# Token lists kept in DRAM instead of one-hot matmuls, in a kernel of linear attention and a mixture of experts on Trainium2

## The chip, the cores and the metric

The kernel runs on one core of one Trainium2 chip. A core has engines that run side by side, each working through its own instructions in order: TensorE (PE, with its weight load PEld) for matmuls, VectorE (DVE), ScalarE (ACT) and GpSimd (POOL) for elementwise work, and SyncE (SP), which here only issues DMAs. POOL issues the indirect DMAs, those whose row addresses come from a list. The metric is device microseconds (us) for one launch. Three runs of the kernel before have a median of 1033.31 us (1033.22 to 1034.61).

## What is computed

The input is 16 sequences of 512 tokens, each of D = 256 numbers. Every token is normalised (`xn`) and goes through two blocks, whose outputs are added to the input:

```
q, k = elu(xn @ Wq + bq) + 1, elu(xn @ Wk + bk) + 1      # 16 heads of 16
v = xn @ Wv + bv
attn = (q @ (k^T v) / max(q . sum(k), eps)) @ Wo + bo     # no softmax: linear
shared = swiglu(xn @ w_in.T) @ w_out.T                    # HIDDEN = 512
g_idx = argmax(softmax(xn @ wg.T + gb))                   # one of 2 groups
w_se = top 2 of the 4 experts of that group, by softmax, times the group's probability
h = swiglu(xn @ w1.T)
routed = sum over experts e of  h * w_se[:, e] @ w2[e].T  # two terms are not zero
out = x + attn + shared + routed
```

Each token thus needs one pair of experts out of 12 (six pairs in each of two groups), and two weights.

## The kernel before

**Two phases.** A loop over the 16 sequences computes all but the routed sum. For each token it leaves one row in `h_d` in DRAM: first the 512 numbers of h, then `BASE` = 258 more (input, attention and shared part added up, then the token's two weights); 770 words in all (`ROW`). Then the tiles phase (class `Tiles`, from L931) takes tokens that share a pair of experts, 128 at a time. `rows()` gathers their rows from `h_d` by an indirect DMA (L943), `turn()` transposes the h part (`hb` on ACT, L964; `hT` on DVE, L970 and L976), `sums()` multiplies by both experts' `w2` at once (`py`, L993), adds with the weights (`y`, L1000 and L1003) and scatters the rows to the output (L1006). Up to 75 tiles (`TILES`) may be needed for 8192 tokens in 12 pairs; 67 (`SURE`) are always run, the others only where a pair's count asks for it, which these inputs do not. Tiles go in twos.

**The homes of gathered rows.** The big buffers of the first phase, `qq_all`, `x_all`, `kk_all` and `xn_all`, are used in turn for the rows of two tiles. The first three of them are free before the last sequence ends. So the rows of the first `AHEAD` = 3 twos are gathered early (from 768.48 us), when h is there but the other part of the last sequence's rows is not. When the last store of `gather_last` has landed (795.13 us), all these rows are gathered once more, whole: two twos ahead of the loop over tiles, the third at its first step, behind the rows for `xn_all`.

**One sequence.** In the order of the code for sequence b: `front(b+1)` makes the residual (`res`, POOL, L390), projects keys, queries and router logits (`pk` L412, `pq` L423) and routes (L433 to L515; DVE, with small pieces on POOL). Routing leaves in `hot` a mark for the token's pair, and in `ahead_of` (POOL) a running count for each partition and pair. Then come `summarize` (`pxk` L689), `normalize` of sequence b+2 (its transposed form goes through DRAM: SP stores `xn_d`, loads four blocks `xb`, L258), `hidden_rows` (`phr`, L595: 14 products, by a scheme of seven per half), `key_sum` (`k` and `k2` on POOL, L676 and L677; `pks` on PE, L679), `attend` (`rz`, L748, and `qb`), `hidden` (`phs`, which ends in `hs_all`), `values` and `mix` (`pvk` L708, `pm` L731, `kvo`), and `gather`: four `po` (L768) of twelve matmuls each, added into `res` by DVE (L777) and stored by SP into the rows of `h_d`.

**What sets the order.** A scheduler places instructions on each engine by their dependencies and priorities; some steps are pinned (`keep_in_program_order`, `issue_after`, `high_priority`). The last sequence pins its `pvk` and `pm` between the products of `hidden` (`small_sums`, L697, with a bank of the pool `ps_y`).

**The order of the tokens** is made by the generator `order()` (L806 to L924), which `between()` (L517) steps forward inside sequences 14 and 15. From the counts it works out where each pair's run of tiles starts, then for every token its slot: tile and row in it. To turn slots into lists it makes one-hot marks on DVE, eight token tiles at a time, and multiplies them on PE, adding up in one bank `pi`:

```python
nc.vector.tensor_tensor(lo, count..., row_of..., ALU.is_equal)       # 128 rows
nc.vector.tensor_tensor(at_tile, count..., tile_of..., ALU.is_equal) # 75 tiles
...
tc.keep_in_program_order(nc.tensor.matmul(
    pi, lhsT=los[:, g % 4, t, :], rhs=his[g % 3][:, t].rearrange("p i n -> p (i n)"),
    start=(g + t == 0), stop=(g * TG + t == TT - 1),
))
```

These are 64 matmuls in bf16 (L894) in eight groups. From `pi` come `source` and `goal`, the row to read and to write for each slot, `where` (which experts each tile takes) and `filled`.

Of the kernel before, what the change touches and what calls it, by code (L numbers as in the profile page):

```python
# [10 lines left out]
FP = mybir.dt.float32  # L11
# [10 lines left out]
def block_kernel(  # L22
# [50 lines left out]
    BASE = D + 2  # L73
    ROW = HID + BASE

    SURE, STEP = 67, 4
    AHEAD = 3
    TG = 8
    TR = 5
    assert TT % TG == 0  # L80
# [10 lines left out]

    h_d = dram.tile([TT * P, ROW], FP, name="h_d")

# [101 lines left out]
    def load_expert(i):  # L195
# [21 lines left out]
    before = const.tile([P, P], FP)  # L217
    nc.gpsimd.affine_select(
        out=before, in_=ones, pattern=[[1, P]],
# [4 lines left out]
    for j in range(EG):  # L224
        nc.gpsimd.memset(place[:, :, j : j + 1], float(j))
    BF = mybir.dt.bfloat16
    count = const.tile([P, P], BF)
    nc.gpsimd.iota(count, pattern=[[1, P]], base=0, channel_multiplier=0,
                   allow_small_or_imprecise_dtypes=True)
    number = const.tile([P, TT], BF)  # L230
    nc.gpsimd.iota(number, pattern=[[1, TT]], base=1, channel_multiplier=0,
                   allow_small_or_imprecise_dtypes=True)
    row = const.tile([P, 1], FP)
    nc.gpsimd.iota(row, pattern=[[0, 1]], base=0, channel_multiplier=1,
# [150 lines left out]
    def residual(b):  # L385

        res = work.tile([P, NT, BASE], FP, tag="res", name=f"res_{b}")
        xt = xs.pop(b)
        for t in range(NT):
            nc.gpsimd.tensor_tensor(res[:, t, 0:D], xt[:, t, :], bo_sb, ALU.add)  # L390
        return res
# [41 lines left out]
    def route(b, lg, res):  # L433
# [75 lines left out]
        for i in range(2):  # L509
            nc.vector.tensor_reduce(  # L510
                res[:, :, D + i : D + i + 1],
                parts[:, i].rearrange("p (t g) c -> p t (g c)", g=G), AX.X, ALU.add,
            )
# [3 lines left out]
    def between(b, n):  # L517

        if b + 2 >= B:
            for _ in range(n or 0):  # L520
                next(steps_of_order)
# [68 lines left out]
    def hidden_rows(b, xs7, then):  # L590
# [16 lines left out]
        seven(f"phr_{b}", product, lambda a: a, room, done, lambda n: between(b, then(n)))  # L607
# [89 lines left out]
    def small_sums(b, shape, name):  # L697

        if b + 1 == B:
            return ps_y.tile(shape, FP, tag="py", name=f"{name}_{b}"), tc.keep_in_program_order  # L700
        return ps_mm.tile(shape, FP, tag="mm", name=f"{name}_{b}"), lambda step: step
# [25 lines left out]
    def mix(b, vk):  # L727
# [7 lines left out]
        with tc.high_priority() if b + 1 == B else nullcontext():  # L735
            nc.scalar.copy(kvo, pm)
# [22 lines left out]
    def outputs(b, t, qT, kvo, hs):  # L759
# [6 lines left out]
        parts += [(qT[:, c, ts(t, P)], kvo[:, c, :]) for c in range(KD)]  # L766
        for i, (a, w) in enumerate(parts):
            nc.tensor.matmul(po, lhsT=a, rhs=w, start=(i == 0), stop=(i == len(parts) - 1))  # L768
        return po

    def gather(b, res, qT, kvo, hs, placed, then):

        for t in range(NT):
            po = outputs(b, t, qT, kvo, hs)

            with tc.issue_after(placed.ins) if placed and t > 1 else nullcontext():
                nc.vector.tensor_tensor(res[:, t, 0:D], po, res[:, t, 0:D], ALU.add)  # L777
            nc.sync.dma_start(out=h_d[ts(b * NT + t, P), HID:ROW], in_=res[:, t, :])
            between(b, then(t))

    def gather_last(b, res, qT, kvo, hs):
# [15 lines left out]
        for i, po in enumerate(pos):  # L797
            to = res[:, 2 * i : 2 * i + 2, 0:D]
# [7 lines left out]
    def order():  # L806

        I32, U32 = mybir.dt.int32, mybir.dt.uint32
        total = keep.tile([P, NP], FP)
        nc.vector.tensor_copy(total, ahead_of[:, TT, :])  # L810
        pc = ps_mm.tile([P, 2 * NP], FP, tag="mm", name="pc")
        tc.keep_in_program_order(
            nc.tensor.matmul(pc[:, 0:NP], lhsT=before, rhs=total, start=True, stop=True)
        )
        nc.tensor.matmul(pc[:, NP:], lhsT=ones, rhs=total, start=True, stop=True)
        pcs = keep.tile([P, 2 * NP], FP)
# [3 lines left out]
        nc.vector.tensor_scalar(ci, pcs[:, NP:], float(P - 1), None, ALU.add)  # L820
# [5 lines left out]
        nc.vector.tensor_copy(runs[0][:, PAD:], ci)  # L826
        for i, d in enumerate((1, 2, 4, 8)):
# [3 lines left out]

        off = keep.tile([P, NP], FP)
        nc.vector.tensor_tensor(off, pcs[:, 0:NP], starts, ALU.add)
        sl = one.tile([P, TT, NP], FP, tag="low", name="sl")
        nc.vector.tensor_tensor(
            sl, ahead_of[:, 0:TT, :], off.unsqueeze(1).to_broadcast([P, TT, NP]), ALU.add
        )
        nc.vector.tensor_tensor(sl, sl, hot, ALU.mult)
        slot = keep.tile([P, TT], I32)
        slf = keep.tile([P, TT], FP)  # L840
        nc.vector.tensor_reduce(slf, sl, AX.X, ALU.add)
        nc.vector.tensor_copy(slot, slf)
        part = keep.tile([P, 2, TT], I32)
        nc.vector.tensor_scalar(part[:, 0, :], slot, P - 1, None, ALU.bitwise_and)
        nc.vector.tensor_scalar(part[:, 1, :], slot, 7, None, ALU.arith_shift_right)
        place_of = keep.tile([P, 2, TT], BF)
        nc.vector.tensor_copy(place_of, part)
# [12 lines left out]
        nc.vector.tensor_copy(where, of)  # L860
        yield


        pi = ps_y.tile([P, 2 * TILES], FP, tag="py", name="pi")

        los = x_all.rearrange("p b t d -> p (b t d)").bitcast(BF).rearrange("p (n t j) -> p n t j", t=TG, j=P)
        his = [
            a[:, B % 2].rearrange("p t d -> p (t d)").bitcast(BF)[:, 0 : TG * 2 * TILES].rearrange(
                "p (t i n) -> p t i n", t=TG, i=2
            )  # L870
            for a in (qq_all, kk_all, xn_all)
        ]

        def marks(g):
            row_of, tile_of = (place_of[:, i, ts(g, TG)].unsqueeze(2) for i in range(2))
            lo, hi = los[:, g % 4], his[g % 3]
            nc.vector.tensor_tensor(
                lo, count.unsqueeze(1).to_broadcast([P, TG, P]), row_of.to_broadcast([P, TG, P]),
                ALU.is_equal,
            )  # L880
            at_tile = one.tile([P, TG, TILES], BF, tag="at_tile", name=f"at_tile_{g}")
            nc.vector.tensor_tensor(
                at_tile, count[:, 0:TILES].unsqueeze(1).to_broadcast([P, TG, TILES]),
                tile_of.to_broadcast([P, TG, TILES]), ALU.is_equal,
            )
            nc.vector.tensor_tensor(
                hi[:, :, 0, :], at_tile,
                number[:, ts(g, TG)].unsqueeze(2).to_broadcast([P, TG, TILES]), ALU.mult,
            )
            nc.vector.tensor_scalar(hi[:, :, 1, :], at_tile, row, None, ALU.mult)  # L890

        def add(g):
            for t in range(TG):
                tc.keep_in_program_order(nc.tensor.matmul(  # L894
                    pi, lhsT=los[:, g % 4, t, :], rhs=his[g % 3][:, t].rearrange("p i n -> p (i n)"),
                    start=(g + t == 0), stop=(g * TG + t == TT - 1),
                ))


        for g in range(TT // TG + 2):  # L900
            if g > 1:
                add(g - 2)
                yield
            if g < TT // TG:
                marks(g)
                yield
        pis = keep.tile([P, 2, TILES], FP)
        nc.vector.tensor_copy(pis.rearrange("p i n -> p (i n)"), pi)
        free = keep.tile([P, TILES], FP)
        nc.vector.tensor_scalar(free, pis[:, 0, :], 0.0, float(2 * TT * P), ALU.is_equal, ALU.mult)  # L910
        tok = keep.tile([P, TILES], FP)
        nc.vector.scalar_tensor_tensor(
            tok, pis[:, 0, :], float(P), pis[:, 1, :], ALU.mult, ALU.add
        )
# [6 lines left out]
        nc.vector.tensor_scalar(source, tok, float(-P), 0.0, ALU.add, ALU.max)  # L921
        goal = keep.tile([P, TILES], U32)
        nc.vector.scalar_tensor_tensor(goal, tok, float(-P), free, ALU.add, ALU.add)
# [5 lines left out]
    rows_of = [a.rearrange("p a b c -> p (a b c)") for a in (qq_all, x_all, kk_all, xn_all)]  # L929

    class Tiles:  # L931
# [6 lines left out]
        def rows(self):  # L938
# [8 lines left out]
            return self  # L947

# [33 lines left out]
        def sums(self):  # L982

            for j, i in enumerate(self.tiles):
# [7 lines left out]
                for f in range(KH):  # L992
# [5 lines left out]
                base = self.hg[:, j, HID:ROW]  # L998
                y = work.tile([P, D], FP, tag="y", name=f"y_{i}", bufs=4)
                nc.vector.scalar_tensor_tensor(  # L1000
                    y, py[:, 0, :], base[:, D : D + 1], base[:, 0:D], ALU.mult, ALU.add
                )
                nc.vector.scalar_tensor_tensor(  # L1003
                    y, py[:, 1, :], base[:, D + 1 : D + 2], y, ALU.mult, ALU.add
# [29 lines left out]
    for b in range(B):  # L1034
# [4 lines left out]
        if b + 2 == B:  # L1039
# [4 lines left out]
            steps_of_order = order()  # L1044
        if b + 1 == B:
            sums7 = token_sums(b, xnT)
            hidden_rows(b, sums7, {2: 2, 6: 2, 9: 2, 13: 2}.get)
# [3 lines left out]
            *lists, filled = next(steps_of_order)  # L1051
            tiles = [Tiles(list(range(i, min(i + 2, SURE))), *lists) for i in range(0, SURE, 2)]
        xk = summarize(b, xn, kk)
# [9 lines left out]
        elif b + 1 < B:  # L1063
            sums7 = token_sums(b, xnT)
            hidden_rows(b, sums7, {9: 1}.get)
# [5 lines left out]
        if b + 2 == B:  # L1071
            next(steps_of_order)
# [3 lines left out]
        if b + 1 < B:  # L1076
            hs, made = hidden(b, sums7) if b else first_hidden(xnT)
            kvo = mix(b, values(b, xk, ksb))
# [11 lines left out]
        if b + 2 == B:  # L1090
            next(steps_of_order)
# [5 lines left out]
        else:  # L1097
            gather(b, res, qT, kvo, hs, normed[b + 2][2]() if b + 2 < B else None, {0: 2, 1: 2, 3: 2}.get)
# [8 lines left out]

# [57 lines left out]
```

## Time and profile before

| | us |
|---|---|
| median of three runs | 1033.31 |
| profiled execution | 1033.23 |
| its span, first to last instruction | 1031.5 |
| granted TensorE clock in it, mean | 0.998 |
| first stage, 0 to 31.5: PE busy | 23.9 |
| sequences 2 to 13, 121.3 to 692.07: PE busy | 569.4 of 570.8 |
| after the last matmul, 1023 to 1031.5: PE busy | 0 |

The span and the profiled execution differ by 1.73 us, which lie around the instructions. The profile gives for each engine its busy time, and for each idle stretch what ended it. A line names the source line, the output, the inputs, their tile and how often. Busy times of matmuls are pipelined: one instruction's duration (mean 592 ns for `py`) is longer than the distance to the next, so what a matmul costs its engine is read from the starts of its neighbours. The clock of TensorE is full in every stage until the tail, so differences of time are not differences of clock.

DMAs move 116.08 MB. The store of `res` (60 of 129 KB) lands 1.9 us after its issue, the four `xb` loads of a sequence 2.8 us after theirs, and the scatter of `y` by POOL 3.0 us after.

### The profile page before, as it was taken

To read this page: it belongs to the slowest core of one execution; us is meant where nothing else is said; L and a number is where in the kernel's file an instruction comes from. 1 tells how busy PE (TensorE), PEld (TensorE's weight loads), DVE (VectorE), ACT (ScalarE), POOL (GpSimd) and SP (SyncE) were. 2 spreads that over 40 slices of the span, in tenths; PEclk is the share of its full clock that TensorE was granted. 3 is DMA by queue.
4 is the path that set the end of the run, shared out by engine and by line. 5 is a ranking of instruction groups with operands and counts; after the bars stand their busy time and mean duration, and the time that the engine had idled before them with its cause. 6 is when DMAs were issued, how large, how long until landed. Compare 5 with 4: busy or idle time off the path is not lost. (4 is left out here: it accounts for less than half of the span.)

```text
span 1031.5 us, 12407 instructions
## 1 busy us (share of the span) xinstructions
PE 1004.9 (97%) x3704; PEld 681.7 (66%) x3704; DVE 779.4 (76%) x1974; ACT 488.1 (47%) x893; POOL 254.8 (25%) x359
## 2 busy tenths in 40 slices
PE   7999999999999999999999999999899999999996
PEld 5466868677786868686777768686667344444442
DVE  5978687878778787878787877868975776666663
ACT  3525353535445253535343534425136576766671
POOL 5302020111202021110202020201012766555652
PEclk9999999999999999999999999999999999999999
DMA  7063534525152522314141313221235755555440
GB/s 220 16 177 107 141 104 101 147 59 154 51 163 54 161 84 81 122 42 143 37 128 56 110 55 123 72 77 61 62 110 146 225 172 153 147 156 157 150 147 30
DMA packets 130339, 116.08 MB, mean 113 GB/s; under 512 B 72637, under 2 KB 114109, under 8 KB 130272
## 3 DMA queue, kind: packets, MB, share of 16 engines
q1 hardware_dynamic: 120064, 77.43, 25.7%
q0 software_dynamic: 9392, 37.58, 12.2%
q8 instruction: 31, 0.51, 0.2%
q10 hardware_dynamic: 816, 0.27, 0.2%
q14 instruction: 36, 0.29, 0.1%
HBM read 65.36 MB, written 50.27 MB: 112 GB/s over the span
## 5 line engine op out<-in xcount | busy, mean ns | idle before, releaser
L993 PE MATMUL py<-w_sb,hT 128*128 x536 | 230.7, 592 | 1.7 <-DVE hT L976 1.6
L993 PEld LDWEIGHTS py<-w_sb,hT 128*128 128x128 f32 x536 | 101.7, 190 | 130.1 <-issue 129.1
L768 PE MATMUL po<-wout_sb,hs_all 128*128 128x256 f32 x480 | 116.6, 380 | 1.4 <-DVE hs_all L580 1.4
L390 POOL TENSOR_TENSOR res<-x_all,bo_sb 128x256 f32<-128x256 f32 x64 | 48.5, 792 | 274.4 <-DMA h_d<-res 203.4
L768 PEld LDWEIGHTS po<-wout_sb,hs_all 128*128 128x128 f32 x480 | 89.2, 190 | 15.1 <-DVE hs_all L580 3.4
L1006 POOL DMA_INDIRECT out<-y,goal x67 | 67.8, 1012 | 76.3 <-DVE y L1003 65.3
L676 POOL TENSOR_TENSOR k<-kk_all 128x512 f32<-128x512 f32 x16 | 20.9, 1307 | 258.3 <-DVE sm L458 247.7
L777 DVE TENSOR_TENSOR res<-po,res 128x256 f32<-128x256 f32 x60 | 25.4, 424 | 76.6 <-PE po L768 76.5
L398 ACT ACTIVATE km<-km 128x1024 f32<-128x1024 f32 x16 | 16.9, 1057 | 138.7 <-DVE km L397 134.4
L595 PE MATMUL phr_w<-w_sb,ss 128*128 128x512 f32 x120 | 61.5, 594 | 2.2 <-DVE ss L538 1.9
L768 PE MATMUL po<-kvo,qT 128*128 128x256 f32 x240 | 61.7, 383 | 0.0
L621 PE MATMUL phs_w<-ss,win_sb 128*128 128x256 f32 x240 | 61.6, 379 | 0.0
L621 PE MATMUL phs_t<-xnT,win_sb 128*128 128x256 f32 x240 | 61.6, 379 | 0.0
L595 PE MATMUL phr_t<-w_sb,xnT 128*128 128x512 f32 x120 | 61.3, 593 | 0.0
L595 PE MATMUL phr_t<-w_sb,ss 128*128 128x512 f32 x120 | 59.4, 597 | 0.0
L621 PE MATMUL phs_t<-ss,win_sb 128*128 128x256 f32 x240 | 59.1, 379 | 0.0
L689 PE MATMUL pxk<-kk_all,xn_all 128*128 128x256 f32 x256 | 58.0, 379 | 0.0
L412 PE MATMUL pk<-wkr_sb,xnT 128*128 128x266 f32 x240 | 57.2, 387 | 0.0
L423 PE MATMUL pq<-w_sb,xnT 128*128 128x256 f32 x240 | 54.2, 379 | 0.0
L689 PEld LDWEIGHTS pxk<-kk_all,xn_all 128*128 128x128 f32 x256 | 48.5, 190 | 6.7 <-issue 0.2
L964 ACT COPY hb<-qq_all 32x256 f32<-32x256 f32 x108 | 43.4, 402 | 17.1 <-DMA qq_all<-h_d,source 9.7
L412 PEld LDWEIGHTS pk<-wkr_sb,xnT 128*128 128x128 f32 x240 | 45.4, 190 | 8.0
(216 smaller groups left out, 1966.0 us busy)
## 6 DMA issues: line engine op xcount, KB each, us to landing
h_d<-hr SPq DMA_DIRECT2D x64, 256.0 KB, 2.5
q_d<-qq_all SPq DMA_DIRECT2D x16, 512.0 KB, 2.8
qb<-q_d SPq DMA_DIRECT2D x64, 128.0 KB, 3.1
w_sb<-in_w SPq DMA_DIRECT2D x64, 128.0 KB, 3.5
h_d<-res SPq DMA_DIRECT2D x60, 129.0 KB, 1.9
x_all<-in_x SPq DMA_DIRECT2D x15, 512.0 KB, 4.8
xn_d<-xn_all SPq DMA_DIRECT2D x14, 512.0 KB, 3.9
xb<-xn_d SPq DMA_DIRECT2D x56, 128.0 KB, 2.8
```

What stands on the lines that cost most here:

```text
L390: nc.gpsimd.tensor_tensor(res[:, t, 0:D], xt[:, t, :], bo_sb, ALU.add)
L412: nc.tensor.matmul(pk, lhsT=xnT[:, k, ts(t, P)], rhs=wkr_sb[:, k, :], start=(k == 0), stop=(k == KD - 1),)
L423: nc.tensor.matmul(pq[:, t, :], lhsT=xnT[:, k, ts(t2 + t, P)], rhs=wq_sb[:, k, :], start=(k == 0), stop=(k == KD - 1),)
L595: tc.keep_in_program_order(nc.tensor.matmul(to, lhsT=xs7[i][:, ts(u, P)], rhs=w1_in[W7[i]], start=start, stop=stop, skip_group_check=True,))
L621: tc.keep_in_program_order(nc.tensor.matmul(split(to)[:, f, :], lhsT=win_in[W7[i]][:, ts(2 * u + f, P)], rhs=xs7[i], start=start and f == ...
L676: nc.gpsimd.tensor_tensor(k2, kk[:, 0:2, :], kk[:, 2:4, :], ALU.add)
L689: nc.tensor.matmul(pxk[:, c, :], lhsT=xn[:, t, ts(c, P)], rhs=kk[:, t, :], start=(t == 0), stop=(t == NT - 1),)
L768: nc.tensor.matmul(po, lhsT=a, rhs=w, start=(i == 0), stop=(i == len(parts) - 1))
L777: nc.vector.tensor_tensor(res[:, t, 0:D], po, res[:, t, 0:D], ALU.add)
L964: nc.scalar.copy(there[ts(q, Q), a - near, 0:n, :], self.hg[ts(a, Q), 0:n, ts(q, W)])
L993: nc.tensor.matmul(py.rearrange("p j d -> p (j d)"), lhsT=self.hT[:, f, ts(j, P)], rhs=w2_sb[:, f, bass.ds(regs[i % TR], 2 * D)], start=(f ...
L1006: stored = nc.gpsimd.indirect_dma_start(out=out_rows, out_offset=bass.IndirectOffsetOnAxis(ap=self.goal[:, i : i + 1], axis=0), in_=y, in_ ...
```

## The change

**Lists by pair, kept in DRAM while the loop runs.** `lists_d` holds, for each of the 12 pairs, 64 rows of 128 entries, and some rows beyond; an entry is one 4-byte word with the token's number, with seven unused words after it. `clear_lists()` fills them once, after sequence 0's `hidden`, with a number beyond all tokens: one memset on POOL and seven DMAs on SP. `enlist(b)` gives every token of a sequence its rank among the tokens of its pair, by two small bf16 matmuls (`pr`), turns it into an address on DVE, and POOL puts each token's number there, 128 at a time. It is called for the next sequence after `attend`, in sequences 1 to 14; the lists of sequences 0 and 1 are made in 1 and 2. The arrays `before` and `ones_bf`, its left operands, are bf16.

**The order.** `order()` is now called at the end of sequence 14. From the counts (`pc`, one bf16 matmul) it works out for each tile which row of `lists_d` it is, gathers these 75 rows (4 KB each) with one indirect DMA, takes every eighth word and transposes the result on PE. Marks, slots, the 64 matmuls and `between()` are gone.

**Sequence 14** places `pvk` and `pm` as sequence 15 does, and its `po` begin with the attention's part.

**Rows** hold the weights first, then the other 256 numbers, then one word of padding (`ROW` = 771 = 3 × 257), so that their last third can be gathered alone. POOL clears the padding in each sequence.

**A fifth home,** `hs_all`, takes rows in turn. The second gathers of the first three twos take only the last 257 words of each row (`bases()`), and stand behind the rows for `xn_all` and `hs_all`.

The core of the diff:

```diff
+    def enlist(b):
+        pr = ps_y.tile([P, NT, NP], FP, tag="py", name=f"pr_{b}")
+        flat = pr.rearrange("p t c -> p (t c)")
+        mine = hot[:, ts(b, NT), :]
+        nc.tensor.matmul(flat, lhsT=before, rhs=mine.rearrange("p t c -> p (t c)"), start=True, stop=False)
+        nc.tensor.matmul(
+            flat, lhsT=ones_bf, rhs=ahead_of[:, ts(b, NT), :].rearrange("p t c -> p (t c)"),
+            start=False, stop=True,
+        )
+        rk = small.tile([P, NT, NP], FP, tag="rk", name=f"rk_{b}")
+        nc.vector.tensor_tensor(rk, pr, lists_at.unsqueeze(1).to_broadcast([P, NT, NP]), ALU.add)
+        nc.vector.tensor_tensor(rk, rk, mine, ALU.mult)
+        rf = small.tile([P, NT], FP, tag="rf", name=f"rf_{b}")
+        nc.vector.tensor_reduce(rf, rk, AX.X, ALU.add)
+        spot = small.tile([P, NT], U32, tag="spot", name=f"spot_{b}")
+        nc.vector.tensor_scalar(spot, rf, float(WORDS), None, ALU.mult)
+        for t in range(NT):
+            put = nc.gpsimd.indirect_dma_start(
+                out=entries,
+                out_offset=bass.IndirectOffsetOnAxis(ap=spot[:, t : t + 1], axis=0),
+                in_=ids[:, b * NT + t : b * NT + t + 1], in_offset=None,
+            )
...
     def small_sums(b, shape, name):
-        if b + 1 == B:
+        if b + 2 >= B:
             return ps_y.tile(shape, FP, tag="py", name=f"{name}_{b}"), tc.keep_in_program_order
...
     def outputs(b, t, qT, kvo, hs):
...
+        if b + 2 == B:
+            parts = parts[KH:] + parts[:KH]
...
     def order():
+        pc = ps_y.tile([P, NP], FP, tag="py", name="pc")
+        nc.tensor.matmul(pc, lhsT=ones_bf, rhs=ahead_of[:, TT, :], start=True, stop=True)
...
+        got = work.tile([P, P * WORDS], U32, tag="blocks", name="got")
+        nc.gpsimd.indirect_dma_start(
+            out=got[0:TILES, :], out_offset=None, in_=lists_d,
+            in_offset=bass.IndirectOffsetOnAxis(ap=part[0:TILES, :], axis=0),
+        )
+        tokens = keep.tile([P, P], FP)
+        nc.vector.tensor_copy(
+            tokens[0:TILES, :], got[0:TILES, :].rearrange("p (n w) -> p n w", w=WORDS)[:, :, 0]
+        )
         yield
-        def marks(g):
...
-        def add(g):
...
+        pi = ps_y.tile([P, TILES], FP, tag="py", name="pi")
+        nc.tensor.transpose(pi, tokens[0:TILES, :], ident[0:TILES, 0:TILES])
...
+    rows_of.append(hs_all.rearrange("p a b -> p (a b)"))
...
+        def bases(self):
+            for j, i in enumerate(self.tiles):
+                nc.gpsimd.indirect_dma_start(
+                    out=self.hg[:, j, HID + 2 :], out_offset=None,
+                    in_=h_d.rearrange("r (a w) -> (r a) w", w=LAST),
+                    in_offset=bass.IndirectOffsetOnAxis(ap=lasts[:, i : i + 1], axis=0),
+                )
...
+        if 0 < b < B - 1:
+            enlist(b + 1)
...
+            if b == 0:
+                clear_lists()
+            elif b < 3:
+                enlist(b - 1)
...
+    EARLY = len(rows_of) - 1
+    for w in tiles[AHEAD:EARLY]:
         w.rows()
     for g, w in enumerate(tiles):
-        if g + AHEAD < len(tiles):
-            tiles[g + AHEAD].rows()
+        if g + EARLY < len(tiles):
+            tiles[g + EARLY].rows()
...
         if g == 0:
-            tiles[AHEAD - 1].rows()
+            for v in tiles[:AHEAD]:
+                v.bases()
```

## The prediction

> **What bounds the kernel now.** I read the busy times first, then TensorE's waits, then busy time by stage, then the timelines of single stages.
>
> The page opens with the span and each engine's busy time, share and count:
>
> ```profile
> span 1031.5 us, 12407 instructions
> ...
> PE 1004.9 (97%) x3704; PEld 681.7 (66%) x3704; DVE 779.4 (76%) x1974; ACT 488.1 (47%) x893; POOL 254.8 (25%) x359
> ```
>
> TensorE is idle for 26.6 us only. 7.6 us are the loading at the start (31.5 − 23.9 busy in the first 31.5 us), 8.5 us the tail after its last matmul. What is left sits mostly in three places. The view of TensorE's waits names them (total, times, longest, in us):
>
> ```profile
> PE pm L731 <- DVE rz L748: 2.5, 1, 2.5
> PE phr_w L595 <- DVE ss L538: 1.9, 1, 1.9
> PE py L993 <- DVE hT L976: 1.6, 1, 1.6
> PE po L768 <- DVE hs_all L580: 1.4, 5, 0.3
> ```
>
> The first two are in sequences 14 and 15, where the order is made; the third is in the tiles phase. Busy time by stage (stage, length, then PE, PEld, DVE, ACT, POOL busy) for sequence 14, for 15, for the tiles:
>
> ```profile
> 692.07:744.50 52.43, 49.73 (x223) 38.06 (x222) 47.67 (x117) 17.33 (x27) 6.23 (x10) 1.00 0.18 58
> 744.50:789.80 45.30, 43.06 (x203) 32.22 (x201) 34.74 (x66) 21.67 (x45) 5.80 (x6) 1.00 0.45 128
> 789.80:1023.00 233.20, 230.71 (x537) 101.50 (x536) 149.90 (x361) 153.78 (x386) 132.00 (x133) 1.00 0.50 152
> ```
>
> An undisturbed sequence is 47.35 us: from pks at 667.24 to the next at 715.03 are 47.79, of which 0.45 are pc. Stage 14 takes 5 us more, with DVE at 47.67 of 52.43 us: it makes the one-hot marks there. So time is won where TensorE executes less, or where DVE stops being late for it.
>
> **What goes.** TensorE's timeline (start, duration, line, operands, count) around pc and the first group of pi:
>
> ```profile
> 711.15 0.29 PE L813 MATMUL pc<-total,before 128*128 128x12 f32 x2
> 711.29 0.37 PE L815 MATMUL pc<-total,ones 128*128 128x12 f32 x2
> 711.51 1.10 PE L595 MATMUL phr_w<-w_sb,ss 128*128 128x512 f32 x2
> ...
> 735.49 0.69 PE L894 MATMUL pi<-qq_all,x_all 128*128 128x150 bf16 x8 [0.23 <-DVE qq_all L890]
> 736.02 1.50 PE L768 MATMUL po<-wout_sb,hs_all 128*128 128x256 f32 x6
> ```
>
> 1. The 64 matmuls of pi: a group of 8 occupies 736.02 − 735.49 = 0.53 us, not 8 times its pipelined duration. Eight groups are 4.3 us, plus about 0.05 each on the instruction behind, 0.4: **−4.7**.
> 2. pc in fp32: 711.51 − 711.15 = 0.36, and 0.09 on the phr pair behind (0.95 against 0.86): 0.45. The single bf16 matmul that replaces it lies between one pi spacing, 0.07, and half of this row, 0.22; I take 0.13, near pi for its type: **−0.3**.
> 3. Waits that the marks and route cause in sequences 14 and 15: pm 2.47 (goes twice over: DVE is freed, and pvk and pm of sequence 14 move later, as 15 has them), phr_w 1.91, one more of phr 0.33, pi 0.23: **−4.9**. What is late next there is hs_all, which holds five po's for 1.4 us in all; it stays.
> 4. The 1.59 us before py of the fourth tile pair. Now its rows come after four whole second gathers; then they are issued first (795.13, in place of 800.15), and second gathers of 257 words stand behind. DVE's order has three y's in front of those transposes, and they wait for these second gathers: by the spacing of 1.25 us the x ones are issued at about 802.7, land 4.3 us later (795.13 to 799.43 below), so y is through at 807.9, the transposes (1.78 + 1.1) at 810.8; TensorE asks at 810.5. About 0.4 is left: **−1.2**.
>
> Sum **−11.1**.
>
> **What comes.**
>
> 5. 16 times pr, two bf16 matmuls of 48 columns with their weight loads. Below, two spacings of the pi row, 2 × 0.067 = 0.13; above, the fp32 pc row, 0.45. I take 0.22, near pi since the type is that: **+3.5** (2.1 to 7.2). Here a rule is weighed: the Trainium skill's "TensorE: Matmul & The Clock Gate", section "Back-to-back issue gap", gives about 81 ns for each load and matmul of 128 columns in a sustained stream, so 32 would be 2.6. A pair alone between fp32 work doesn't overlap like a stream, so I stay above it; a run of the changed kernel will tell.
> 6. The order's new chain. pc now comes after the last phs of sequence 14; some twenty DVE operations of 12 to 60 columns follow, a gather of 75 rows of 4 KB, a copy, and a transpose on TensorE that stands between po_3 of sequence 14 and the first phr of 15. Put on sequence 13's times (last phs at 679.75): offsets done at 686–687, gather 4.3, copy 0.25, so ready at 690.4–691.4. TensorE has four po's of 2.59 and pc: free at 690.2. Wait **+0.8** (0; or 6.6, if the landing takes the 9.9 us that is the longest of such a gather in the trace). The transpose itself: **+0.35** (as pt).
> 7. Sequence 1: the queue of SP now has the store of res_1, which waits for po, before the transfers of xb for sequence 3. Its xnT is then ready about 122.5 by my count of the queue, pk wants it at 121.75: **+0.8** (0 to 2, most of the 2.45 us that one such transfer takes). Queued behind on SP are also the eight w2 loads, wanted much later.
> 8. pm of sequences 1 and 2 stands two matmuls earlier: 0.15 each, **+0.3**.
>
> Sum **+5.75**.
>
> **Costed at nothing.** Four DVE operations of 0.19 us per sequence for rank and address, 0.75 us: DVE has 0.33 + 0.44 + 0.42 = 1.19 us idle at 674–677; behind, from 677.4 to 684.9, it has none, and po waits for it. Without that cover, 14 × 0.75 = 10.5. The 64 puts of 128 entries: POOL issues a gather every 1.25 us, so 5 us per sequence, with POOL idle 75%; behind them stands only k of the next sequence, which pks needs at 667.24 and which is ready at 656.08: 11 us of slack. A put waits for its address on POOL; behind it the same k. Clearing 3.2 MB by seven DMAs: SP is idle from 79.6 to 95.7 us. The word of padding per row and its memset: POOL, idle. Some normalising operations of later sequences move ahead on DVE and one table load on ACT; both engines do the same work in all.
> Against the puts speaks a rule of the skill, "DMA: Bandwidth & Descriptors", section "Anatomy of one DMA — SWDGE (gpsimd) path": a fixed 2.0 us for each DMA, 128 us for 64 if serial. The trace's nearest row, the scatter of y, occupies POOL for 1.01 us each and lands after 3.0; nobody waits for a put until the list is read 30 us after the last. By either price nothing is on the path.
>
> **The sum.** −11.1 + 5.75 = −5.35. The profiled execution took 1033.23 (span 1031.5 and 1.73 around it); the median of the three runs, 1033.31, is the same within 0.1. Forecast **1027.9 us**. Less: pr at 2.1, no wait for the list, none for xb: −8.4, 1024.8. More: the three high ends of 5, 6 and 7 add 3.7 + 5.8 + 1.2 and give 1038.6; together they are unlikely.
>
> **Rivals.**
>
> A, **slower**: a put disturbs DVE. In sequence 14 a POOL operation and a small DVE one ran together:
>
> ```profile
> 701.28 1.31 POOL L676 TENSOR_TENSOR k<-kk_all 128x512 f32<-128x512 f32 x1 [3.17 <-DVE sm L458]
> ...
> 701.62 1.02 DVE L467 TENSOR_TENSOR pe<-ex,sm 128x32 f32<-128x32 f32 x1
> ```
>
> That pe takes 0.18 elsewhere: 0.84 lost. If each of four puts costs DVE 0.8, and its slack is 1.19, then 3.2 − 1.19 = 2.0 us in each of 14 sequences: +28, about 1055. It decides from 1.6 us of delay per sequence, two such hits (14 × 0.4 eats the gain). The skill's "SBUF — State Buffer" says that DVE and GpSimd share a port pair under an exclusive lock and the loser blocks; by this, puts could hurt. Against it, an indirect DMA beside a DVE operation with two SBUF inputs:
>
> ```profile
> 769.82 0.97 POOL L943 DMA_INDIRECT qq_all<-h_d,source  x1 [0.30 <-issue]
> ...
> 769.96 0.42 DVE L722 TENSOR_TENSOR vk<-vk,headmask 128x256 f32<-128x256 f32 x1
> ```
>
> It took 0.42, as at 682.28 with POOL idle. The put is of this kind, so I cost it at zero. A part of A is that the 0.75 us doesn't fit in DVE's gaps.
>
> B, **no change**: the list lands late, +5.8, or pr costs 0.55 each, +5.3: about 1033. For: the longest landing is 9.9. Against: the queue of POOL is nearly empty then, and the gather that these lines show took 4.3 from its issue to the y that waited for it:
>
> ```profile
> 795.13 0.95 POOL L943 DMA_INDIRECT qq_all<-h_d,source  x1 [19.32 <-DMA h_d<-res]
> ...
> 799.43 0.48 DVE L1000 SCALAR_TENSOR_TENSOR y<-py,qq_all 128x256 f32<-128x256 f32 x1 [7.80 <-DMA qq_all<-h_d,source]
> ```
>
> C, **larger gain**: pr at two spacings, no wait for the list: 1024.5. For: both are lower bounds that rows show. Against: the DVE chain has to be done within 7 us with no slip.
>
> That the change doesn't do what it says is excluded: in the instruction order of the changed kernel the 64 matmuls of pi and their marks are gone.
>
> **How the numbers follow.** Forecast 0.60, C 0.10, B 0.11, A 0.19. A measurement of this kernel tells changes over about 0.2%, 2.1 us. Faster: forecast and C, 0.70. Same: B, 0.11. Slower: A, 0.19. The range leaves out the far part of A (above 1036, about 0.14) and a little below: 1024.0 to 1036.0, which takes in C, B and the mild part of A.
>
> **What would show it.** Step 1: no pi group, and stage 14 near 47 us. Step 3: pm and phr_w gone from the waits. Step 4: hT's wait under 0.6. Step 5: the spacing from pr's start to the matmul behind it, 0.22. Step 6: a wait of pi for tokens under 2 us. Step 7: a wait of pk near 122 us. A: waits of po for hs_all, or of pks for k2, that repeat in every sequence, and DVE rows whose means grow. The forecast is wrong if such repeated waits exceed 0.4 us per sequence, or the list lands over 6 us late.

## The result and the profile after

The changed kernel takes 1035.95 us (median of twelve runs, 1034.69 to 1037.52), the kernel before, beside it on the same chip, 1033.99: a ratio of 1.0018, with a 95% interval of 1.0009 to 1.0026. A second comparison gave 1.0017 (1.0010 to 1.0023). So the change costs about 1.9 us, where 5.4 us of gain were forecast.

The page of the changed kernel opens with the span and the busy times:

```profile
span 1033.4 us, 12508 instructions
...
PE 1002.8 (97%) x3670; PEld 680.0 (66%) x3670; DVE 768.4 (74%) x2001; ACT 480.9 (47%) x887; POOL 323.8 (31%) x442
```

TensorE executes 2.1 us less than before and DVE 11 us less; POOL is busy 69 us more (the puts take 72). The span is 1.9 us longer all the same. Where that lies shows when both executions are cut at the same work. The rows give the stage, its length, then PE, PEld, DVE, ACT and POOL busy, clock, DMA share and GB/s. The cuts are the key sum of sequence 2, that of sequence 14, the first `py`, the first `y` of the last tile, and the end. Before:

```profile
0.00:96.47 96.47, 87.18 (x300) 56.70 (x301) 76.78 (x239) 37.37 (x57) 29.83 (x78) 1.00 0.42 120
96.47:667.24 570.77, 569.36 (x2330) 431.58 (x2329) 452.24 (x1165) 249.23 (x367) 79.93 (x131) 1.00 0.35 101
667.24:789.84 122.60, 117.66 (x541) 91.91 (x540) 100.31 (x212) 47.72 (x86) 12.03 (x16) 1.00 0.31 94
789.84:1022.24 232.40, 230.67 (x537) 101.48 (x535) 149.13 (x360) 153.74 (x386) 132.00 (x133) 1.00 0.50 152
1022.24:1031.50 9.26, 0.00 (x0) 0.00 (x0) 0.96 (x2) 0.00 (x0) 0.98 (x1) 0.74 0.03 11
```

After:

```profile
0.00:96.95 96.95, 87.50 (x301) 57.08 (x302) 77.01 (x239) 37.28 (x57) 30.71 (x83) 1.00 0.51 140
96.95:674.65 577.70, 572.88 (x2358) 433.08 (x2357) 466.08 (x1221) 242.37 (x361) 139.09 (x199) 1.00 0.38 102
674.65:786.89 112.24, 112.24 (x479) 87.92 (x478) 76.02 (x183) 47.49 (x86) 21.76 (x26) 1.00 0.38 105
786.89:1017.13 230.24, 230.20 (x537) 101.88 (x535) 148.35 (x360) 153.79 (x386) 131.25 (x133) 1.00 0.49 147
1017.13:1033.40 16.27, 0.00 (x0) 0.00 (x0) 0.96 (x2) 0.00 (x0) 0.98 (x1) 0.62 0.02 8
```

Line by line the lengths change by +0.5, +6.9, −10.4, −2.2 and +7.0 us. Up to the last tile the changed kernel is 5.1 us ahead (1017.13 against 1022.24), within 0.3 us of the forecast's 5.4. Then it loses 7.0 us in the last stage, in which TensorE and ACT do nothing, DVE and POOL work for 1 us each at its start, and the DMA engines are nearly idle (share 0.02). The prediction set nothing for that row.

What stands in it is seen by asking the trace for the program's closing instructions (line, engine, operation, count; shortest, median and longest in ns; first and last start). Two of them grow: `INC_SWDGE_SEM`, which stands on the line where POOL jumps over the tiles that aren't needed, and the first and longest of POOL's three drains (`DRAIN`), right behind it. Before:

```profile
L1121 POOLq INC_SWDGE_SEM  x1: 1007/1007/1007, 1026.2 to 1026.2; - x1
L1161 POOLq DRAIN  x3: 51/103/3418, 1027.2 to 1031.2; - x3
```

After:

```profile
L1137 POOLq INC_SWDGE_SEM  x1: 2316/2316/2316, 1021.5 to 1021.5; - x1
L1177 POOLq DRAIN  x3: 51/103/8727, 1023.9 to 1033.1; - x3
```

The drain took 3.4 us and takes 8.7, +5.3. The step before it takes 2.3 us in place of 1.0, +1.3. Together they are 6.6 of the 7.0 us. All other engines have finished their work.

TensorE's waits after the change, for comparison with those of before (us in total, times, longest):

```profile
PE phr_w L640 <- DVE hr L619: 2.0, 6, 0.4
...
PE po L815 <- DVE hs_all L625: 1.4, 5, 0.3
PE pk L424 <- DVE xnT L275: 1.0, 1, 1.0
PE pm L776 <- DVE rk L552: 0.4, 2, 0.2
```

The waits of `pm` for `rz`, of `phr_w` for `ss` and of `py` are gone. New are six short ones of `phr_w`, one of `pk`, and two of `pm`.

### The profile page after: what moved, and what is told of

It reads as the page before. It is cut to its first block, busy times and chain, and to the rows that moved or that the text cites. A ratio compares the mean times of both kernels' runs of the same rounds, so it can differ in the third digit from the quotient of the medians.

```text
span 1033.4 us, 12508 instructions
## 1 busy us (share of the span) xinstructions
PE 1002.8 (97%) x3670; PEld 680.0 (66%) x3670; DVE 768.4 (74%) x2001; ACT 480.9 (47%) x887; POOL 323.8 (31%) x442
## 4 chain that ended last, share of the span: by engine, by line
PE 78%; DVE 13%; DMA 4%; issue 2%; ACT 1%; SPq 1%; POOL 1%; DVEq 0%; ACTq 0%; POOLq 0%
PE py L996 22%; PE po L815 13%; PE phs_t L666 8%; PE phr_t L640 6%; PE pk L424 5%; PE pq L435 5%; PE phs_w L666 4%; PE phr_w L640 4%; PE pxk L734 3%; PE phr_l L640 2%; PE phs_l L666 2%; PE pm L776 1%; DVE xn_all L301 1%; PE phs L708 1%; PE po L834 1%
## 5 line engine op out<-in xcount | busy, mean ns | idle before, releaser
L559 POOL DMA_INDIRECT lists_d<-ids,spot x64 | 72.4, 1131 | 184.7 <-DVE spot L557 157.3
```

What stands on the lines that cost most here:

```text
L559: put = nc.gpsimd.indirect_dma_start(out=entries, out_offset=bass.IndirectOffsetOnAxis(ap=spot[:, t : t + 1], axis=0), in_=ids[:, b * NT + ...
```

## The experiments

Two theories stood against each other. P: the puts lengthen POOL's end, since a drain takes time for each indirect DMA that no drain has taken yet. Q: the end is longer for another reason. The first four kernels ran on a chip on which the kernel before took 1040.32 us, not 1033 to 1034 as elsewhere; each is compared with the kernel before on its own chip, and what is read from their traces is the end.

**A drain in sequence 15.** POOL idles there for 20 us.

```diff
             for w in tiles[:AHEAD]:
                 w.rows()
+            with tc.issue_after(tiles[AHEAD - 1].last.ins):   # the last of these gathers
+                nc.gpsimd.drain()
```

> The changed kernel with one more drain of POOL, in sequence 15, behind the six early gathers (POOL is idle there from 772 to 792 us). Theory P (POOL's closing drain takes time for every indirect DMA that no drain has taken yet, and the 64 puts lengthen it): the new drain takes about 80 of the 214 DMAs, the closing one falls from 8.7 to about 3.4 us and the semaphore step before it from 2.3 to about 1.0, as before the change; total 6.6 us less, about 1029.3. Rival Q (the end is longer for another reason, such as the code's length behind the last branch): the closing drain stays at 8.7, total about 1036.

Measured: 1038.69 us, ratio 0.9984 (0.9977 to 0.9991). The closing drain fell to 2.3 us and the step before it to 0.8, somewhat lower than said. The changed kernel itself did not run on this chip, so the 6.6 us can't be measured there; 1.6 us under the kernel before is less than the 4.7 to be expected. The execution has one wait of `py` for `hT` of 8.9 us in the tiles phase, of which no run of the changed kernel on another chip shows anything; all four traces of this chip have one there, of 4.7 to 8.9 us, and its cause stays open. Q is out for the end itself.

**Puts alone.** The kernel before, with puts nobody needs, ordered behind each sequence's count; the instructions of TensorE, DVE and ACT keep their order.

```diff
+    def extra_puts(b):
+        for t in range(NT):
+            for to in spare_d:                # one array, or two for 128 puts
+                with tc.issue_after(counted[b].ins):
+                    put = nc.gpsimd.indirect_dma_start(
+                        out=to, out_offset=..., in_=row[:, 0:1], in_offset=None)
...
+        if b + 1 < B:
+            extra_puts(b + 1)
```

> The kernel before, with 64 puts of 128 words of 4 bytes into an array nobody reads, four in each sequence behind the count of that sequence; the order is made as before. Theory P: PE's last matmul is where it was (1022.2), the closing drain grows from 3.4 to about 8.7 us and the step before it from 1.0 to 2.3: total about 1040.6. Rival Q: total 1034, the end unchanged. Rival A of the prediction (puts disturb DVE): PE ends later than 1022.2, by 2 us a sequence at the price given there.

Measured: 1050.97 us, 1.0110 (1.0093 to 1.0126). The closing instructions:

```profile
L1183 POOLq DRAIN  x3: 51/103/8645, 1038.9 to 1048.1; - x3
```

8.65 us, as the changed kernel has; the step before it 2.29. So puts alone make the longer end, without anything else of the change. The time grew by 10.7, not 6.6. Against the trace of before, from the other chip, the key sum of sequence 2 is 1.8 us late (the puts of two sequences fall together there); up to sequence 15 (717.43) only 0.6 us more are lost, where rival A of the prediction set 2 us for each sequence. The remaining 2 us or so stay unexplained; the tiles phase of this chip has the waits named above.

> The same with 128 puts, eight in each sequence. Theory P, linear: 13.2 us over the kernel before, about 1047, with a closing drain of about 14 us. Theory P with a bound (the count of untaken DMAs cannot pass some number near 128, or is taken when that is reached): the closing drain is at most about what 64 puts give, or falls back to a few us. Rival Q: 1034.

Measured: 1053.22 us, 1.0125 (1.0107 to 1.0144), and a closing drain of 5.2 us:

```profile
L1183 POOLq DRAIN  x3: 51/103/5215, 1046.1 to 1051.9; - x3
```

With twice the puts the drain is SHORTER than with 64. The linear form of P falls; what remains is a bound. The time is still 2.2 us longer than with 64, since TensorE ends 8.1 us later (1040.7 against 1032.6): among its waits are now five of `phs_t` for ACT's `r_phs`, 5.0 us in all.

**Drains through the tiles phase,** one behind every fourth two of tiles besides that of sequence 15:

```diff
         w.sums()
+        if g % 4 == 3 and g + 1 < len(tiles):
+            with tc.issue_after(w.stored.ins):
+                nc.gpsimd.drain()
```

> The changed kernel with the drain of sequence 15 and one more behind every fourth two of tiles. Theory P: only the last six DMAs are left for the closing drain, which then is below 1 us, and the step before it about 0.5: about 10 us less than the changed kernel, 1026, if the drains in the tiles phase (each waits for the landing of the last DMA, 3 us, and takes about 30 at 0.08, 2.4 us) stay hidden behind the four twos of rows gathered ahead; PE's waits for hT would show if not. Rival Q: 1036 or more.

Measured: 1037.01 us, 0.9968 (0.9960 to 0.9976). Closing drain 0.28 us, step before it 0.26. The end is taken away; the time is clouded by the same 8.5 us wait of `py` on this chip. (Three DMAs stand behind the last drain, not six.)

**The changed kernel again, and parts of it undone,** on another chip, to see which steps carried the 5.1 us.

> The changed kernel once more, unaltered, beside the others on one chip. By the first comparison 2 us over the kernel before (ratio 1.0018), closing drain 8.7 us, PE's last matmul 5 us earlier than before the change.

Measured: 1035.29 us, ratio 1.0017, closing drain 8.7: the result stands.

```diff
-        if b + 2 >= B:
+        if b + 1 == B:      # small_sums; likewise kvo's priority, the order of po's parts, and the call
```

> The changed kernel with sequence 14's pvk, pm and po where they were before the change. If taking the marks off DVE alone removes the wait of pm for rz (2.5 us before), the time is that of the changed kernel within 0.5 us; if the place of pm does it, pm waits again and the time is up to 2.5 us longer. My prediction counted this wait as removed twice over.

Measured: 1037.39 us, 2.1 us over the changed kernel beside it. The wait is back, under another name:

```profile
PE pm L776 <- DVE pcs L856: 2.0, 1, 2.0
```

The name misleads: `pcs` is a copy of 0.16 us that merely ended last. `pm` reads `vk`, and its last operation on DVE,

```profile
737.17 0.42 DVE L767 TENSOR_TENSOR vk<-vk,headmask 128x256 f32<-128x256 f32 x1
```

has to wait for two additions for `hs_all`, of 0.68 us each, that DVE does after `pvk` is there. In the kernel before it was the same: `vk` ended at 730.98, and only behind it, at 731.01, did DVE start on the first marks. So the marks were not what `pm` waited for, and without them 2.0 of its 2.5 us are left. Placing `pvk` and `pm` earlier, with the three steps that go with it, removes the wait.

```diff
-    rows_of.append(hs_all.rearrange("p a b -> p (a b)"))
...
-    EARLY = len(rows_of) - 1      # and the loop over tiles as before the change
```

> The changed kernel with four homes and second gathers of whole rows, as before the change (rows keep their new layout). If the fifth home takes away py's wait for hT, that wait is back at about 1.6 us and the time is 1.2 to 1.6 us longer; if not, no difference. POOL issues as many DMAs as the changed kernel, so the closing drain stays near 8.7 us.

Measured: 1037.13 us, 1.8 us over the changed kernel, with the wait back:

```profile
PE py L995 <- DVE hT L978: 1.4, 2, 1.1
```

The fifth home and the shorter second gathers do what the prediction said, and a little more.

**Two orders pinned,** besides the drains:

```diff
+            with tc.issue_after(blocks_in["xb", b + 2].ins) if b == 1 else nullcontext():
                 nc.sync.dma_start(out=h_d[ts(b * NT + t, P), HID:ROW], in_=res[:, t, :])
...
-            with tc.issue_after(last_xn[-1].ins) if last_xn else nullcontext():
+            with tc.issue_after(routed[b - 1].ins):
                 for t in range(g, g + n):
                     nc.vector.bn_stats(out=st[:, t, :], in_=xt[:, t, :])
```

> The changed kernel with the drains of the run before (one in sequence 15, one behind every fourth two of tiles), and two orders pinned: in sequence 1 the stores of res stand behind the four xb loads on SP, and the normalising of b+2 stands behind the routing of b+1 on DVE. If the early losses are what the trace says, PE's wait for xnT (1.0, and 0.3 behind it) goes and the six waits of phr_w for hr (2.0, and 0.05 behind each) go: 3.5 us less than the drains alone; with them (tail 9 us shorter than the changed kernel) 12 us less than the changed kernel, 10 less than the kernel before. Rival: another stage is late at once (the normalised rows reach DRAM later, xb late), then the gain of the orders is under 1 us.

Measured: 1063.42 us, 1.0284 (1.0267 to 1.0302): a clear miss. TensorE waits for ACT again and again:

```profile
PE phs_t L667 <- ACT r_phs L613: 17.4, 24, 1.2
PE phr_t L641 <- ACT hr L619: 15.7, 11, 2.0
```

A likely reading is that the later normalising makes ACT's square root, which waits for it, stand in front of the copies that free TensorE's banks; this wasn't tested further. The first pin alone does no harm, as two later runs show. The second does what it was for: the six waits of `phr_w` for `hr` are gone from this trace. What it brings in their place costs 33 us, so it is no remedy.

**Is the bound a matter of luck?** 149, 213, 214 and 277 DMAs seemed to fit multiples of 107.

```diff
+        if b == 3:
+            for t in range(NT):       # four puts into spare_d, behind the count of the sequence
```

> The changed kernel with four MORE puts of 4-byte words (into an array nobody reads, in sequence 2; PE, DVE, ACT and SP keep their order). The closing drains so far lie on 0.0817 us times what is left of POOL's DMAs after taking away whole multiples of 107: 149 leave 42 (3.43, measured 3.42), 213 leave 106 (8.66; 8.65), 214 stand at the brim (8.74; 8.73), 277 leave 63 (5.15; 5.22). By this rule 218 DMAs leave 4: a closing drain of 0.3 us, the step before it 0.3, and a time 10.4 us under the changed kernel, 8.5 under the kernel before. Rival: the drain grows with every DMA, and only the run with 128 puts was odd; then 9.1 us and 0.3 us more than the changed kernel.

Measured: 1035.66 us, 1.0021 (1.0014 to 1.0028). The rule failed and its rival held to the digit:

```profile
L1191 POOLq DRAIN  x3: 51/103/9053, 1023.8 to 1033.4; - x3
```

9.05 us is 0.326 more than 8.73, for four DMAs: 0.0815 us for each.

> The same, and sequence 1's stores of res stand behind the four xb loads on SP. If that order is what delays xnT, PE's wait of 1.0 to 1.5 us for it goes, with 0.1 to 0.3 behind it: 1.2 to 1.7 us less than with four more puts alone, 10 under the kernel before. If the run with both orders pinned gained or lost by this one too, it shows here alone.

Measured: 1034.30 us, 1.0005 (0.9996 to 1.0014): 1.4 us under the run with four more puts alone, and `pk` no longer waits for `xnT`. The order of SP's queue was worth what it was said to be; the end stayed at 9.05.

> The kernel BEFORE with a drain of POOL behind every fourth two of tiles. Closing drain 3.4 to 0.3, the step before it 1.0 to 0.3: 3.8 us less than the kernel before, if the drains stay hidden behind three twos of rows gathered ahead. If they don't, PE waits for hT and the time is longer.

Measured: 1030.76 us, 0.9967 (0.9953 to 0.9981), closing drain 0.28. So the kernel before carried a part of this too, 3.4 us of drain. With only three twos of rows ahead the drains are not quite hidden: `py` waits 2.8 us in four pieces where it waited 1.6.

**The rule of the bound, and the sum without the end.**

> The changed kernel with 28 more puts (four in each of sequences 2 to 8), 242 DMAs in all. The run with a drain in sequence 15 left 134 DMAs behind it and had a closing drain of only 2.3 us: so by the time that 134 are held, about 107 of them are taken without a drain. If that is the rule, 242 DMAs pass that point a second time (107 + 134 = 241) and leave 28: closing drain about 2.3 us, the step before it 0.8, and a time 8 us UNDER the changed kernel, with more puts than it. If the closing drain grows with every DMA, 11.0 us and 2.9 us more than the changed kernel.

Measured: 1031.75 us, 0.9983 (0.9976 to 0.9989), against 1.0018 for the changed kernel: with 28 more useless puts it is faster by some 3.6 us. Its end:

```profile
L1191 POOLq DRAIN  x3: 51/103/2351, 1026.6 to 1029.5; - x3
```

2.35 us, as expected, and the step before it 0.75. The 8 us of the expectation were not reached in time because TensorE ended 4.7 us later (1021.8 against 1017.1): with eight puts in a sequence `po` waits 3.7 us for `hs_all` in place of 1.4, `pk` 2.2 for `xnT` in place of 1.0, and 0.7 for `res`.

> The changed kernel with the drains (sequence 15, and behind every fourth two of tiles) and sequence 1's stores of res behind the four xb loads. PE's last matmul where the changed kernel with that order has it (about 1016.3 to 1016.6, 5 us before the kernel before), closing drain 0.3 us, the step before it 0.3: 5.5 us from the last DMA's issue to the end in place of 8.0: about 1024.7, 8.8 us under the kernel before (ratio 0.9915). If the drains hold POOL back so that rows come late, PE waits for hT, and the gain is smaller by that.

Measured: 1024.06 us, ratio 0.9906 (0.9890 to 0.9923), the fastest of all. The row of its end:

```profile
1015.67:1022.30 6.63, 0.00 (x0) 0.00 (x0) 0.97 (x2) 0.00 (x0) 0.98 (x1) 0.86 0.10 34
```

6.6 us from the last tile's `y` to the end, in place of 16.3. The drain of sequence 15 takes 18 us and those of the tiles phase 3.4 to 7.0, all beside TensorE's work: with five homes `py` waits for nothing. The kernel before with drains had 0.9967; from there to 0.9906 are about 6.3 us, 1.4 of them for the order of SP's queue. That leaves 4.9 us for the change itself once neither kernel pays for its end, or some 4 without the 1.2 us that `py` waits longer in the former: an estimate from medians on two chips.

All ends together, with the number of DMAs that POOL issued since the start or since the last drain, counted in the order of the program (nine of those since the start are plain loads):

| kernel | DMAs since then | closing drain, us | step before it, us |
|---|---|---|---|
| before | 149 | 3.42 | 1.01 |
| puts alone, 64 | 213 | 8.65 | 2.29 |
| changed | 214 | 8.73 | 2.32 |
| four more | 218 | 9.05 | 2.40 |
| 28 more | 242 | 2.35 | 0.75 |
| puts alone, 128 | 277 | 5.22 | 1.45 |
| changed, drain in sequence 15 | 134 | 2.33 | 0.76 |
| changed, drains in the tiles phase | 3 | 0.28 | 0.26 |

From 149 to 218 the drain lengthens by 0.082 us for each DMA; so does it from 242 to 277 (2.87 for 35). Between 218 and 242 it falls by 6.7 us, which is 82 DMAs' worth, though 24 were added: some 106 have been taken on the way, without a drain. The same has happened before the 134th of the run with a drain in sequence 15. It has happened once in the kernel before, too: its 3.42 us are 42 DMAs' worth, not 149. And with 218 the 9.05 us are 111 DMAs' worth, so that many can be held. That POOL takes about 106 by itself when a bound between 111 and 134 is reached, and a drain goes through what is left, fits every row; what POOL does inside was not observed. Nor is it shown which DMAs a closing drain goes through: by this reading a put counts only as one more, and those left at the end may all be of the tiles phase.

## Why the prediction was wrong

**The step that failed** is "Costed at nothing": of the 64 puts it said "nobody waits for a put until the list is read 30 us after the last. By either price nothing is on the path." Somebody does wait: the program's end. From 149 DMAs to 214 each one adds 0.082 us to POOL's closing drain and 0.020 to the step before it, 6.6 us for 65 DMAs (the puts and the gather of the list), though the puts landed hundreds of microseconds earlier. The prediction priced what a put costs its engine and its queue; it took the 8.5 us behind the last matmul as fixed and did not ask what they consist of. The drain of 3.4 us was in the trace of before to be read. That 1035.95 lies below the upper end of the stated range, 1036.0, is luck: that end was meant for puts that disturb DVE.

**The rest of the sum was right in total, in part by luck:** −5.35 forecast to the last tile, −5.1 measured. Costs set too high (pr by 1.3 us, the list by 0.8, its transpose by about 0.2, what is left of `py` by 0.4) made up for 2.3 us of `phr_w` and 0.4 of `pm` that were set at nothing. By its own steps:

1. pi: gone, as forecast.
2. pc: one bf16 matmul, as forecast. The start of the next group lies 0.03 behind it, and that group is 0.08 longer than the others of its kind (0.94 to the next start, where they take 0.86): 0.11 where 0.13 was set. The list's transpose:

```profile
747.05 0.28 PE L907 MATMUL pi<-ident,tokens 75*128 75x75 f32 x1
747.17 1.07 PE L640 MATMUL phr_t<-w_sb,xnT 128*128 128x512 f32 x2
```

It costs 0.12 to the next start and about 0.05 behind it, where 0.35 was set.

3. The waits of sequences 14 and 15: gone. But "waits that the marks and route cause" was a wrong reading for `pm`, and "goes twice over" with it: DVE's additions for `hs_all` held `vk`, and only the earlier place removes the wait, as the run with it undone showed.
4. `py` for `hT`: the forecast left 0.4; nothing is left (undone, 1.4 comes back).
5. pr: sized 0.22, measured 0.14. The view is TensorE's timeline again:

```profile
722.57 0.19 PE L546 MATMUL pr<-hot,before 128*128 128x48 bf16 x1
722.60 0.18 PE L547 MATMUL pr<-ahead_of,ones_bf 128*128 128x48 bf16 x1
722.62 1.11 PE L666 MATMUL phs_t<-xnT,win_sb 128*128 128x256 f32 x4
```

0.05 for the pair and 0.09 for the next group; a sequence takes 47.90 us where it took 47.76. The lower bound, two spacings of pi (0.13), was near; 16 pairs cost 2.2, not 3.5. The 2.6 us worked out from the Trainium skill ("TensorE: Matmul & The Clock Gate", "Back-to-back issue gap"), an estimate for 128 columns where pr has 48, came nearer than the 3.5; the reason given for staying above it, that a lone pair overlaps less, did not hold here.

6. The list: ready just in time. `tokens` is written at 747.00 (from 746.73 on, in 0.27), and TensorE is free of the last `po` at 747.02; no wait where 0.8 was set.
7. `xnT`: 1.0 to 1.5 us, and 1.4 came back when the order was mended: right in mechanism, sized at 0.8.
8. `pm` in sequences 1 and 2: right, but it also waits 0.18 twice for `rk`, which the forecast left out.

A second step was wrong and was covered by these: "Some normalising operations of later sequences move ahead on DVE ...; both engines do the same work in all." The same work, but beside other work of POOL, and there it takes longer. The two views give the count, the busy time in us and the mean in ns of the normalising operation, before and after:

```profile
L290 DVE TENSOR_SCALAR xn_all<-x_all,mv,rs 128x256 f32<-128x256 f32 x56 | 31.2, 557 | 0.0
L301 DVE TENSOR_SCALAR xn_all<-x_all,mv,rs 128x256 f32<-128x256 f32 x56 | 44.6, 797 | 0.0
```

In six early sequences the four operations of a sequence took 0.40 us each before; now each runs while POOL works on `k` or `res`, and they take 1.24, 0.82, 0.87 and 0.91. So DVE comes later to the addition that frees a bank for `phr_w`: six waits of 0.34 us, with 0.05 behind each, 2.3 us in all. The run with the second pin bears this out: there the operation takes 407 ns in the mean, and the six waits are gone.

One sum was wrong as well: rival C's two terms, 1.4 us less for pr and 0.8 for the list, give 1025.7, not 1024.5.

**Rival A** priced a put at up to 0.8 us of DVE's time. In the changed kernel the means of DVE's largest operations do not move (the additions of `r_phr` and `hr` are 688 ns both times, the product with `rz` 1223), `po` waits for `hs_all` as often as before, and where a put meets that product, POOL gives way:

```profile
680.38 1.23 DVE L795 TENSOR_TENSOR qq_all<-qq_all,rz 128x1024 f32<-128x1024 f32 x1
...
680.65 1.82 POOL L559 DMA_INDIRECT lists_d<-ids,spot  x1 [12.05 <-DVE spot L557]
682.77 0.96 POOL L559 DMA_INDIRECT lists_d<-ids,spot  x1 [0.30 <-issue]
```

Beside a DVE operation with two inputs this put takes 1.82 us, the next one 0.96. The first put takes 1.74 to 1.85 us in twelve sequences, each time beside this operation of DVE, which keeps its 1.22. So of the two that share a pair of ports by the Trainium skill's "SBUF — State Buffer", section "SBUF: two separate sides", POOL is the loser here, and POOL has time. The operation that grew most, the normalising, did so beside `k` and `res`; with the 64 puts alone its mean stayed at 557 ns, and the four of its operations that ran beside a put took 0.32 to 0.41. With eight puts in a sequence a delay did begin, as the runs with 28 more and with 128 show; whether DVE itself was held there or POOL's own work came late wasn't separated. Rival A's side, slower, came true by a mechanism that no rival named.

## What to carry to other kernels

Work that is off the critical path can still be on the path of the program's end: ask what every queue must settle before the launch is over, and read the last microseconds of the trace, instruction by instruction, before calling a DMA free. Where POOL issues many indirect DMAs, count them, and let it drain where it idles. A scheduler's side effect, even "the same work in another order", has to be followed to the operations it now runs beside, and to the wait it makes.

## What the hardware showed unexpectedly

POOL's closing drain lengthens by 0.082 us for each DMA that POOL issued since the start or the last drain (149 to 218 of them: 3.4 to 9.1 us), though the last of them had landed before the drain began (in the changed kernel at 1021.2, against 1023.9). Somewhere between 111 and 134 held, about 106 go without a drain; so adding 28 puts shortened it from 8.7 to 2.4 us. A put that met DVE's product with `rz` took 1.8 us in place of 0.96, and DVE lost nothing; a normalising operation of DVE that met POOL's `k` took 1.24 us in place of 0.40.
